# An adaLN transformer block on one core: the feed-forward's modulation moved from TensorE to VectorE, the first gate alone on TensorE, and the second half of x loaded ahead of the rotary tables

## The chip, the cores and the metric

The kernel runs on 1 core of a Trainium2 chip. The metric is the device time of one execution in microseconds (us). Five engines work beside each other, each through its own queue in order: TensorE (PE, and PEld for its weight loads), VectorE (DVE), ScalarE (ACT), GpSimd (POOL) and SyncE (SP), which issues most of the DMA transfers.

## The reference: what is computed

x is 2 x 1024 x 256 in float32 (two batches, 1024 tokens). A vector c per batch is turned into six rows of 256: shift, scale and gate for the attention (sa, ca, ga) and for the feed-forward (sb, cb, gb).

```
mod = (silu(c) @ wmod).reshape(2, 6, 1, 256)
sa, ca, ga, sb, cb, gb = (mod[:, n] for n in range(6))
ga = (2 * (ga >= 0) - 1) * maximum(abs(ga), 0.25)        # gb likewise
h = layernorm(x) * (1 + ca) + sa
x = x + ga * attention(h, Wq, bq, Wk, bk, Wv, bv, Wo, bo)  # 16 heads of 128, rotary, causal
h = layernorm(x) * (1 + cb) + sb
x = x + gb * ffn(h)                       # silu(gate) * up, then down; 704 hidden, integer weights
```

## The kernel before

Everything is float32 but the integer weights. Rows of x lie in 8 tiles of 128 tokens per batch. A *head* below is one of the 32 units (batch, group of two heads, head), numbered 0 to 31 as the loop `for n, u in enumerate(units)` (line 754) takes them; each has 8 *slots* `i`, one for each tile of 128 queries. The order of all work is written out by hand (`manual_schedule`, line 700), and each engine's queue runs in that order.

In a slot the loop issues, in this order: `shared_out` (one output product `py`, line 516, of an earlier head, whose sum into x is VectorE's line 519; `py` has one PSUM bank, so the next `py` waits for that sum); `score` (the products `ps`, line 429, and VectorE's mask and row maximum `nmax`, line 432); `turned` (VectorE transposes the probabilities of the slot before into `t`, line 463; after every fourth tile SyncE issues 16 transfers that make `pT` of them, line 475); `expo` (ScalarE's exp, line 449); `release` (the rotary sums that the slot before has held back: VectorE's line 402 and GpSimd's line 405); `project_qk` in slots 1, 3, 4, 5 (the next head's q and k, line 386, ScalarE's r1, line 398, GpSimd's product with the sine table, line 399); `values` (the products `po` of probabilities and v, line 490, copied out by ScalarE, line 498: for the first 512 queries of the head before in slot 0, but in slot 2 while n is 1, for its last 512 in slots 6 and 7); `project_v` in slots 0 and 2 (two tiles of v, line 368, copied out by ScalarE, line 375); and `extras`, where everything else is put into a slot by hand: `fold_out` (GpSimd scales Wo by the gate of the attention, lines 337 to 341, in slot 2 of even heads), loads by ScalarE's queue (the second batch's x, the feed-forward's weights `raw` and scales `s_bc`), VectorE's conversion of these weights (line 280), the layernorm of the second batch and of the feed-forward.

Before the loop stands the start. The transfers of the first inputs are issued in the order c (ScalarE's queue), x tiles 0 to 3, the attention's modulation weights `wmod` in two halves, the gates' weights `wga`, Wq and Wk of the first group, the first halves of the rotary tables, x tiles 4 and 5, Wv, x tiles 6 and 7, the second halves of the tables, the feed-forward's modulation weights, the weights of the next group. Some matmuls on ones (`warm_ps`) run ahead. TensorE then makes the attention's shift and scale as columns (`modulation(0)`: 16 matmul records `pm`, line 123), transposes the first four normalized tiles of x (`ptx`, line 216), which VectorE and ScalarE write to `hT` with shift and scale (lines 224 and 222), and makes q, k and v of head 0; the second four tiles follow. `gates_product` (line 147) makes the rows of both gates, 512 wide, its two terms in two places behind the transposes; `gates` (lines 153 to 162) clamps them on VectorE, writes them to DRAM and reads them back into all partitions. The feed-forward's shift and scale are made by `modulation(2)` in slot 7 of head 0, `wmod`'s second half being loaded by then.

Tiles of one tag share buffers: tag `f` has two, which hold first `wmod` and `wga`, then `s_bc` and `raw`, then others. `bw` (fold_out's small tile) has two.

Of the kernel before, what the change touches and what calls it, by code (L numbers as in the profile page):

```python
# [37 lines left out]
def adaln_block(ctx: ExitStack, tc: tile.TileContext, a, cos_d, sin_d, out):  # L38
# [20 lines left out]

    wmod = fpool.tile([P, 2, 2, KC, D], F32, tag="f", name="wmod")  # L60
    wga = fpool.tile([P, KC, 2 * D], F32, tag="f", name="wga")

    def load_x(b, t, n, eng):
        eng.dma_start(x[b][:, t : t + n, :], x_d[b, :, t : t + n, :])

    def load_wmod(block, n, eng):
        eng.dma_start(wmod[:, block, n], a["L0_wmod"][block, n])


    row_c = rot.tile([P, QB], F32, tag="r1", name="row_c")[: B * KC, :P]  # L70
    nc.scalar.dma_start(row_c, a["L0_c"])
    load_x(0, 0, 1, nc.sync)
    load_x(0, 1, 3, nc.sync)
    for n in range(2):
        load_wmod(0, n, nc.sync)

# [37 lines left out]

    def modulation(which, pool, tag):

        pm = pool.tile([P, 512], F32, tag=tag, name=f"pm{which}")

        wide = pm.rearrange("p (n f r b) -> p n f r b", n=2, f=KC, b=B)
        for n in range(2):  # L120
            for f in range(KC):
                for k in range(KC):
                    nc.tensor.matmul(  # L123
                        wide[:, n, f],
                        wmod[:, which // 2, n, k, ts(f, P)],
                        sc[:, :, k].unsqueeze(1).to_broadcast([P, P // B, B]),
                        start=(k == 0),
                        stop=(k == KC - 1),
                    )
        pms[which] = wide  # L130

    pms = {}

    def shift_scale(which):
        pm = pms[which]
        for n in range(2):
            nc.vector.tensor_scalar(modT[:, which + n], pm[:, n, :, 0, :], float(n), None, ALU.add)

    dram = pool("dram", 1, space=bass.MemoryType.DRAM)
    grow_d = dram.tile([B, 2 * D], F32, name="grow_d")  # L140

    pgs = []

    def gates_product(k):
        if k == 0:
            pgs.append(ps_y.tile([P, 512], F32, tag="y", name="pg"))
        nc.tensor.matmul(pgs[0][:B], sc[:, :, k], wga[:, k, :], start=(k == 0), stop=(k == KC - 1))  # L147

    def gates():

        pg = pgs.pop()
        sgn = ppool.tile([P, S], F32, tag="p", name="sgn")[:B, :QB]
        nc.vector.tensor_scalar(sgn, pg[:B], 0.0, 2.0, ALU.is_ge, ALU.mult)
        mag = ppool.tile([P, S], F32, tag="p", name="mag")[:B, :QB]
        nc.vector.tensor_scalar(mag, pg[:B], -1.0, None, ALU.mult)
        nc.vector.scalar_tensor_tensor(mag, pg[:B], 0.25, mag, ALU.max, ALU.max)
# [543 lines left out]
    with tc.manual_schedule():  # L700
        pc = ps_a.tile([P, 512], F32, tag="a", name="pc")
        nc.tensor.transpose(pc[:, : B * KC], row_c, ident[: B * KC, : B * KC])
        for n in range(2):
            warm_up(4)
        nc.scalar.activation(sc.rearrange("p b k -> p (b k)"), pc[:, : B * KC], AF.Silu)
        nc.scalar.activation(warm, eps_t, AF.Sqrt)
        weights[0, 0] = {}
        nc.sync.dma_start(wga, a["w_gates"])
        load_w(0, 0, "q")
        load_w(0, 0, "k")  # L710
        for t, t_d in ((cos_t, cos_d), (sin_t, sin_d)):
# [19 lines left out]
        modulation(0, ps_o, "o")  # L731
        nc.scalar.dma_start(cols, a["biases"])
        ln_scale(0, "a", 0, (0, 1))
        ln_scale(0, "a", 0, (2, 3))
        shift_scale(0)
        ln_turn(0, "a", 0, 0, new_hT(0, 0), split=True)
        gates_product(0)
        for t in range(4, NT):
# [15 lines left out]
        for n, u in enumerate(units):  # L754
            b, g, h = u
            prev = units[n - 1] if n else None
            nxt = units[n + 1] if n + 1 < N else None
            nb, ng = (b, g + 1) if g + 1 < NG else (b + 1, 0)
            more = nb < B
            for i in range(NT):  # L760

                shared_out(8 * n + i - 13)
                if owed:
                    owed.pop()()
                ps, nmax = score(u, i)
                if i >= 1:
                    turned(u, i - 1)
                elif prev:
                    turned(prev, NT - 1)
                expo(u, i, ps, nmax)  # L770
                release()
                if i in (1, 3, 4, 5) and nxt:
                    project_qk(nxt, *{1: ("q", 0), 3: ("k", 0), 4: ("q", 1), 5: ("k", 1)}[i])
                if i in (6, 7) and prev:
                    values(prev, 1, 4 * (i - 6), 4 * (i - 5))
                if i in (0, 2):
                    if h == 0:
                        project_v(b, g, 4 + i, *((ps_a, "a") if n else (ps_o, "o")))
                    elif more:
                        project_v(nb, ng, i)  # L780
                if not nxt and i in filler:
                    hidden(0, 0, filler.index(i), late=False, hold=True)

                if prev and i == (0 if n > 1 else 2):
                    values(prev, 0, 0, 4)
                extras(n, i)
                if i == 7 and h == 1:
                    if more:
                        load_out(nb, ng)
                    if n + 3 < N:  # L790
                        load_proj(*units[n + 3][:2])
# [119 lines left out]
```

## Time and profile before

| | |
|---|---|
| median of 3 runs | 1072.07 us (1071.98 to 1072.41) |
| the profiled execution | 1071.95 us |
| its span, from the first instruction to the last | 1070.2 us |
| start of head 0, 1, 2, 3 on TensorE | 23.13, 42.99, 70.56, 99.83 us |
| length of most heads from then on | 29.27 us |
| VectorE, ScalarE, GpSimd busy in head 2 (29.27 us) | 18.02, 14.35, 14.68 us |
| DMA | 132.02 MB in all, mean 123 GB/s |

A group of the profile reads: line of the kernel, engine, operation, what it writes <- what it reads, partitions x elements; then busy time and the mean of one in ns. In a timeline the first two numbers are the start and the length in us from the span's start, and a bracket at the end holds the engine's idle time before the instruction and what ended it. Matmuls are pipelined, so their records overlap. One product of float32 makes two records. Lengths of a head on TensorE are taken from the starts of its first `ps`.

### The profile page before, as it was taken

Reading aid. Unit: us, or ns where it says so; the run is one execution under the profiler, and the core shown is the slowest. Engines: PE = TensorE matmul, PEld = TensorE weight load, DVE = VectorE, ACT = ScalarE, POOL = GpSimd, SP = SyncE. Lnnn points to the kernel's source line nnn. Section 1 sums busy time; section 2 is a strip of 40 time slices with the busy share of each in tenths; the row PEclk is TensorE's granted clock in tenths of the full one; section 3 lists DMA queues with packets and bytes.
Section 4 is the critical chain, followed back from the end, with each engine's and each line's share of the span. In section 5 each row is a group of like instructions: output and inputs, shape, how many; then the busy total and the mean of one; then the engine's idle time right before and its main releaser. Section 6 shows DMA issues by size and latency. Waiting matters only on the chain.

```text
span 1070.2 us, 12390 instructions
## 1 busy us (share of the span) xinstructions
PE 1066.2 (100%) x3513; PEld 638.2 (60%) x3513; DVE 655.2 (61%) x1427; ACT 507.8 (47%) x956; POOL 398.8 (37%) x368
## 2 busy tenths in 40 slices
PE   9999999999999999999999999999999999999998
PEld 5665655666665655555666666656555666545747
DVE  5665675665667776665776556656767856555321
ACT  5654454554445444544544444544555544562120
POOL 4735353534343343754333444334343333200100
PEclk9999999999999999999999999999999999999999
DMA  6465656656565555566564656454555656423201
GB/s 227 104 159 126 159 120 141 156 126 148 119 150 115 142 119 134 120 148 163 111 148 109 148 116 148 101 138 99 144 121 116 148 129 138 110 50 77 71 1 39
DMA packets 68047, 132.02 MB, mean 123 GB/s; under 512 B 19302, under 2 KB 23402, under 8 KB 67980
## 3 DMA queue, kind: packets, MB, share of 16 engines
q1 hardware_dynamic: 66340, 126.96, 50.1%
q10 hardware_dynamic: 1592, 4.16, 1.2%
q8 instruction: 28, 0.46, 0.2%
q14 instruction: 39, 0.32, 0.1%
q0 software_dynamic: 48, 0.13, 0.1%
HBM read 25.26 MB, written 2.10 MB: 26 GB/s over the span
## 4 chain that ended last, share of the span: by engine, by line
PE 100%; issue 0%; DVE 0%; POOL 0%; POOLq 0%
PE po L490 23%; PE ps L429 23%; PE py L516 10%; PE pv L368 10%; PE pq L386 10%; PE pk L386 10%; PE pgu L545 7%; PE pd L603 2%; PE pd_0w L603 1%; PE pd_1w L603 1%; PE warm_ps L86 1%; PE pm L123 0%; PE pd L592 0%; PE pg L147 0%; PE ptx_a L216 0%; PE pd_1r L603 0%
## 5 line engine op out<-in xcount | busy, mean ns | idle before, releaser
L449 ACT ACTIVATE p<-ps,nmax 128x128 f32<-128x128 f32 (+7 forms) x256 | 189.8, 741 | 343.1 <-DVE nmax L432 342.9
L429 PE MATMUL ps<-kT,qT 128*128 128x512 f32 (+3 forms) x768 | 289.5, 486 | 0.0
L432 DVE CUSTOM_DVE_ANT_0 ps<-ps,mask 128x128 f32<-128x128 f32 (+7 forms) x256 | 195.6, 764 | 114.4 <-PE ps L429 113.6
L490 PE MATMUL po<-pT,v 128*128 128x512 f32 (+3 forms) x768 | 263.6, 486 | 0.0
L519 DVE SCALAR_TENSOR_TENSOR x<-py,rden,x 128x256 f32<-128x256 f32 x256 | 122.9, 481 | 224.5 <-PE py L516 220.9
L490 PEld LDWEIGHTS po<-pT,v 128*128 128x128 f32 x768 | 145.7, 190 | 123.4 <-issue 92.8
L399 POOL TENSOR_TENSOR r_q<-r_q,sin_t 128x512 f32<-128x512 f32 x64 | 81.9, 1279 | 362.5 <-ACT r_q L398 360.4
L463 DVE STREAM_TRANSPOSE t<-p 128x128 f32<-128x128 f32 (+7 forms) x256 | 198.2, 774 | 3.6 <-DMA pT<-t 1.8
L429 PEld LDWEIGHTS ps<-kT,qT 128*128 128x128 f32 x768 | 145.7, 190 | 77.6 <-issue 64.1
L516 PE MATMUL py<-wo,o 128*128 128x256 f32 x512 | 151.2, 380 | 0.0
L516 PEld LDWEIGHTS py<-wo,o 128*128 128x128 f32 x512 | 92.6, 190 | 77.6 <-issue 52.6
L368 PE MATMUL pv<-wv,hT 128*128 128x256 f32 x512 | 121.1, 379 | 0.0
L386 PE MATMUL pq<-hT,wq 128*128 128x512 f32 x256 | 120.5, 593 | 0.0
L386 PE MATMUL pk<-hT,wk 128*128 128x512 f32 x256 | 120.3, 592 | 0.0
L368 PEld LDWEIGHTS pv<-wv,hT 128*128 128x128 f32 x512 | 94.8, 190 | 19.5 <-issue 1.3
L399 POOL TENSOR_TENSOR r_k<-r_k,sin_t 128x512 f32<-128x512 f32 x64 | 81.5, 1273 | 64.5 <-ACT r_k L398 64.3
L405 POOL TENSOR_TENSOR kT<-kT,r_k 128x512 f32<-128x512 f32 x64 | 81.2, 1268 | 56.5 <-DVE kT L402 41.6
L398 ACT ACTIVATE r_q<-pq,cols 64x512 f32<-64x512 f32 x128 | 87.4, 683 | 21.9 <-PE pq L386 19.6
L405 POOL TENSOR_TENSOR qT<-qT,r_q 128x512 f32<-128x512 f32 x64 | 83.4, 1303 | 33.6 <-DVE qT L402 30.9
L398 ACT ACTIVATE r_k<-pk,cols 64x512 f32<-64x512 f32 x128 | 87.4, 683 | 5.9 <-PE pk L386 0.4
L386 PEld LDWEIGHTS pk<-hT,wk 128*128 128x128 f32 x256 | 48.6, 190 | 48.0 <-issue 45.0
L386 PEld LDWEIGHTS pq<-hT,wq 128*128 128x128 f32 x256 | 46.2, 190 | 33.1 <-issue 30.6
(104 smaller groups left out, 686.7 us busy)
## 6 DMA issues: line engine op xcount, KB each, us to landing
pT<-t SPq DMA_DIRECT2D x512, 128.0 KB, 2.4
pT<-t SPq DMA_DIRECT2D x512, 64.0 KB, 2.0
wq<-in_Wq SPq DMA_DIRECT2D x16, 256.0 KB, 3.1
wk<-in_Wk SPq DMA_DIRECT2D x16, 256.0 KB, 4.0
wv<-in_Wv SPq DMA_DIRECT2D x16, 256.0 KB, 4.3
wo<-in_Wo SPq DMA_DIRECT2D x16, 256.0 KB, 2.8
out<-yo SPq DMA_DIRECT2D x15, 128.0 KB, 1.8
wmod<-in_wmod SPq DMA_DIRECT2D x4, 256.0 KB, 4.6
```

The lines of the kernel that those rows point to most:

```text
L368: nc.tensor.matmul(pv[:, ts(j, HG * DH)], hT[b, n][:, k, ts(r, P)], weights[b, g]["v"][:, k, :], start=(k == 0), stop=(k == KC - 1),)
L386: nc.tensor.matmul(pq, weights[b, g][s][:, k, ts(h, DH)], hT[b, n][:, k, :], start=(k == 0), stop=(k == KC - 1),)
L398: nc.scalar.activation(r1[to], pq[of], AF.Identity, bias=cols[of, c : c + 1])
L399: nc.gpsimd.tensor_tensor(r1, r1, sin_t[:, sl], ALU.mult)
L405: nc.gpsimd.tensor_tensor(dst[:, sl], dst[:, sl], r1, ALU.add)
L429: nc.tensor.matmul(ps[:, c:e], qT[:, ts(i, P)], kT[:, c:e], start=True, stop=True)
L432: nc.vector.tensor_tensor_reduce(ps[:, :L], ps[:, :L], mask[:, NT - 1 - i :, :].rearrange("p t k -> p (t k)"), -SCALE, FLT_MAX, ALU.add, A ...
L449: nc.scalar.activation(p[:, :L], ps[:, :L], AF.Exp, bias=nmax, scale=-1.0, accum_out=dens[u][:, i : i + 1])
L463: nc.vector.transpose(t32[blk][:, :, j, : i + 1, :].rearrange("p c k b -> p k c b"), p[:, : (i + 1) * P].rearrange("p (k c a) -> p k c a", ...
L490: nc.tensor.matmul(po[:, off * P :], vs[b, g][:, k, ts(h, DH)], pT[:, off:, :, k, :], start=(k == 0), stop=(k == last),)
L516: nc.tensor.matmul(py[:, :D], outs[u][:, ts(t, P)], weights[b, g]["o"][:, h, :], start=True, stop=True)
L519: nc.vector.scalar_tensor_tensor(x[b][:, t, :], py[:, :D], rdens[u][:, t : t + 1], x[b][:, t, :], ALU.mult, ALU.add)
```

## The change

The attention's modulation (shift and scale) stays with TensorE; its weights and the weights of the first gate are one tile of three parts. The first gate's row is made alone (`gate_a`): 256 wide, both terms in the first of the two places. For the feed-forward, silu(c) is written to DRAM as a row by GpSimd's queue and read back into all partitions; `late_load` (slot 7 of head 1, ScalarE's queue) brings that and the weights, turned so that an output column is a row of 256 in each partition. `late_column` makes one column of shift, scale or gate for both batches with two multiply-and-sum reductions on VectorE, in slots 3 and 5 of heads 2, 3 and 4. The second gate is clamped as columns (`gate_b`, head 5), turned by one transpose on TensorE (`gate_b_turn`, head 6), and spread over the partitions (head 7).

In the order of loads, x tiles 4 to 7 stand ahead of the rotary tables, and Wv behind the tables' first halves; the second batch's x and the feed-forward's weights are loaded in other heads. The v products of group 1 move: two of the four from heads 1 and 2 into slots 6 and 7 of head 0. The first `values` of head 2 go to slot 2.

```diff
-    wmod = fpool.tile([P, 2, 2, KC, D], F32, tag="f", name="wmod")
-    wga = fpool.tile([P, KC, 2 * D], F32, tag="f", name="wga")
+    wmod = fpool.tile([P, 3, KC, D], F32, tag="f", name="wmod")
...
-    def load_wmod(block, n, eng):
-        eng.dma_start(wmod[:, block, n], a["L0_wmod"][block, n])
-    row_c = rot.tile([P, QB], F32, tag="r1", name="row_c")[: B * KC, :P]
+    def load_wmod(n):
+        nc.sync.dma_start(wmod[:, n], a["L0_wmod"][n])
+    row_c = small.tile([P, D], F32, tag="bw", name="row_c", bufs=2)[: B * KC, :P]
...
-    def shift_scale(which):
-        pm = pms[which]
+        return wide
...
-    grow_d = dram.tile([B, 2 * D], F32, name="grow_d")
-    pgs = []
-    def gates_product(k):
-        if k == 0:
-            pgs.append(ps_y.tile([P, 512], F32, tag="y", name="pg"))
-        nc.tensor.matmul(pgs[0][:B], sc[:, :, k], wga[:, k, :], start=(k == 0), stop=(k == KC - 1))
-    def gates():
...
+    crow_d = dram.tile([1, B * D], F32, name="crow_d")
+    grow_d = dram.tile([2, B, D], F32, name="grow_d")
+    late = {}
+    def gates(sgn, mag, pg):
...
-        nc.sync.dma_start(grow_d, mag)
+    def gate_rows(n):
         for b in range(B):
-            for m, n in enumerate(("a", "b")):
-                nc.sync.dma_start(
-                    gate[n, b], grow_d[b : b + 1, m * D : (m + 1) * D].to_broadcast([P, D])
-                )
+            row = grow_d["ab".index(n), b : b + 1, :]
+            nc.sync.dma_start(gate[n, b], row.to_broadcast([P, D]))
+    def gate_a():
+        pg = ps_y.tile([P, 512], F32, tag="y", name="pg")[:B, :D]
+        for k in range(KC):
+            nc.tensor.matmul(pg, sc[:, :, k], wmod[:, 2, k, :], start=(k == 0), stop=(k == KC - 1))
+        def rest():
+            sgn = ppool.tile([P, S], F32, tag="p", name="sgn")[:B, :D]
+            mag = ppool.tile([P, S], F32, tag="p", name="mag")[:B, :D]
+            gates(sgn, mag, pg)
+            nc.sync.dma_start(grow_d[0], mag)
+            gate_rows("a")
+        return rest
+    def late_load():
+        t = fpool.tile([P, (3 * KC + B) * D], F32, tag="f", name="late_mod")
+        late["w"] = t[:, : 3 * KC * D].rearrange("p (n f k) -> p n f k", n=3, f=KC)
+        late["c"] = t[:, 3 * KC * D :].rearrange("p (b k) -> p b k", b=B)
+        nc.scalar.dma_start(t[:, 3 * KC * D :], crow_d.to_broadcast([P, B * D]))
+        nc.scalar.dma_start(late["w"], a["late_mod"])
+        late["g"] = const.tile([P, B, KC], F32, name="gcol")
+    def late_column(n, f):
+        for b in range(B):
+            junk = xnp.tile([P, D], F32, tag="xn", name=f"junk{n}{f}{b}")
+            to = modT[:, 2 + n, f, b : b + 1] if n < 2 else late["g"][:, b, f : f + 1]
+            nc.vector.tensor_tensor_reduce(
+                junk, late["w"][:, n, f], late["c"][:, b], 1.0, float(n == 1), ALU.mult, ALU.add, to
+            )
+    def gate_b():
+        g = late["g"].rearrange("p b f -> p (b f)")
+        sgn = small.tile([P, B * KC], F32, tag="sgn", name="sgn_b", bufs=1)
+        mag = small.tile([P, B * KC], F32, tag="mag", name="mag_b", bufs=1)
+        gates(sgn, mag, g)
+        late["mag"] = mag
+    def gate_b_turn():
+        mag = late["mag"]
+        pt = ps_o.tile([P, 512], F32, tag="o", name="pgb")[: B * KC, :P]
+        nc.tensor.transpose(pt, mag, ident)
+        rows_ = small.tile([P, D], F32, tag="bw", name="grow", bufs=2)[: B * KC, :P]
+        nc.scalar.copy(rows_, pt)
+        nc.sync.dma_start(grow_d[1].rearrange("b (f p) -> (b f) p", p=P), rows_)
...
         if i == (2 if n else 7) and units[n][2] == 0:
             fold_out(*units[n][:2])
-        if n == 0 and i == 7:
-            modulation(2, ps_y, "y")
-            shift_scale(2)
+        if n == 1 and i == 7:
+            late_load()
+        if n in (2, 3, 4) and i in (3, 5):
+            late_column(n - 2, i // 4)
+        if n == 5 and i == 3:
+            gate_b()
+        if n == 6 and i == 3:
+            gate_b_turn()
+        if n == 7 and i == 3:
+            gate_rows("b")
...
-        for m, name in ((3, "gate"), (5, "up"), (6, "last")):
+        for m, name in ((5, "gate"), (6, "up"), (7, "last")):
             if n == m and i == 7:
                 ffn_weight_load(name)
             if n == m + 1 and i in (2, 5):
                 ffn_weight_scale(name, i // 4)
-        if n in (0, 4, 6, 8) and i == 7:
-            load_x(1, max(0, n - 2), 2, nc.scalar)
+        if n in (3, 4, 8, 9) and i == 7:
+            load_x(1, {3: 0, 4: 2, 8: 4, 9: 6}[n], 2, nc.scalar)
...
+        nc.scalar.activation(row_c, row_c, AF.Silu)
         nc.scalar.activation(warm, eps_t, AF.Sqrt)
+        nc.gpsimd.dma_start(crow_d.rearrange("o (r p) -> (o r) p", p=P), row_c)
         weights[0, 0] = {}
-        nc.sync.dma_start(wga, a["w_gates"])
+        load_wmod(2)
         load_w(0, 0, "q")
         load_w(0, 0, "k")
+        load_x(0, 4, 2, nc.sync)
+        load_x(0, 6, 2, nc.sync)
         for t, t_d in ((cos_t, cos_d), (sin_t, sin_d)):
             nc.sync.dma_start(t[:, :QB], t_d[:, :QB])
-        load_x(0, 4, 2, nc.sync)
         load_w(0, 0, "v")
-        load_x(0, 6, 2, nc.sync)
         for t, t_d in ((cos_t, cos_d), (sin_t, sin_d)):
             nc.sync.dma_start(t[:, QB:], t_d[:, QB:])
-        for n in range(2):
-            load_wmod(1, n, nc.sync)
         load_proj(*units[2][:2])
         load_out(0, 0)
         nc.gpsimd.memset(bvacc, 0.0)
...
         ln_turn(0, "a", 0, 0, new_hT(0, 0), split=True)
-        gates_product(0)
+        gate_a_rest = gate_a()
...
         ln_turn(0, "a", 1, 0, new_hT(0, 1), split=True, wide=True)
-        gates_product(1)
         project_v(0, 0, 2, ps_sc, "sc", S)
-        gates()
+        gate_a_rest()
...
                 if i in (0, 2):
-                    if h == 0:
-                        project_v(b, g, 4 + i, *((ps_a, "a") if n else (ps_o, "o")))
+                    if n in (1, 2):
+                        if i == 0:
+                            project_v(0, 1, 2 + 2 * n)
+                    elif n == 0:
+                        project_v(b, n, 4 + i, ps_o, "o")
+                    elif h == 0:
+                        project_v(b, g, 4 + i)
                     elif more:
                         project_v(nb, ng, i)
+                if n == 0 and i in (6, 7):
+                    project_v(0, 1, 2 * (i - 6))
...
-                if prev and i == (0 if n > 1 else 2):
+                if prev and i == (0 if n > 2 else 2):
                     values(prev, 0, 0, 4)
                 extras(n, i)
...
     wmod = v["L0_wmod"].reshape(D, 2, 3, D)
-    args["L0_wmod"] = given("in_wmod", by_partition(np.moveaxis(wmod[:, :, :2], 0, 2), 2))
-    args["w_gates"] = given("in_w_gates", by_partition(wmod[:, :, 2].reshape(D, 2 * D)))
+    args["L0_wmod"] = given("in_wmod", by_partition(np.moveaxis(wmod[:, 0], 0, 1), 1))
+    late_mod = wmod[:, 1].reshape(D, 3, KC, P)
+    args["late_mod"] = given("in_late_mod", late_mod.transpose(3, 1, 2, 0))
```

More of the change, by code (lines that the diff above doesn't have):

```diff
@@ L74, in adaln_block @@
     for n in range(2):
-        load_wmod(0, n, nc.sync)
+        load_wmod(n)
     ident = const.tile([P, P], F32, name="ident")
@@ L113, in adaln_block, with modulation @@
     bvacc = const.tile([P, D], F32, name="bvacc")
-    def modulation(which, pool, tag):
-        pm = pool.tile([P, 512], F32, tag=tag, name=f"pm{which}")
+    def modulation(pool, tag):
+        pm = pool.tile([P, 512], F32, tag=tag, name="pm")
         wide = pm.rearrange("p (n f r b) -> p n f r b", n=2, f=KC, b=B)
@@ L124, in modulation @@
                         wide[:, n, f],
-                        wmod[:, which // 2, n, k, ts(f, P)],
+                        wmod[:, n, k, ts(f, P)],
                         sc[:, :, k].unsqueeze(1).to_broadcast([P, P // B, B]),
@@ L129, in modulation, with shift_scale @@
                     )
-        pms[which] = wide
-    pms = {}
-    def shift_scale(which):
-        pm = pms[which]
+        return wide
+    def shift_scale(pm):
         for n in range(2):
-            nc.vector.tensor_scalar(modT[:, which + n], pm[:, n, :, 0, :], float(n), None, ALU.add)
+            nc.vector.tensor_scalar(modT[:, n], pm[:, n, :, 0, :], float(n), None, ALU.add)
     dram = pool("dram", 1, space=bass.MemoryType.DRAM)
-    grow_d = dram.tile([B, 2 * D], F32, name="grow_d")
-    pgs = []
@@ L144, in gates_product @@
-    def gates_product(k):
-        if k == 0:
-            pgs.append(ps_y.tile([P, 512], F32, tag="y", name="pg"))
-        nc.tensor.matmul(pgs[0][:B], sc[:, :, k], wga[:, k, :], start=(k == 0), stop=(k == KC - 1))
-    def gates():
[L151 to L156, printed above, removed]
+    crow_d = dram.tile([1, B * D], F32, name="crow_d")
@@ L157, in gates @@
+    grow_d = dram.tile([2, B, D], F32, name="grow_d")
+    late = {}
+    def gates(sgn, mag, pg):
+        nc.vector.tensor_scalar(sgn, pg, 0.0, 2.0, ALU.is_ge, ALU.mult)
+        nc.vector.tensor_scalar(mag, pg, -1.0, None, ALU.mult)
+        nc.vector.scalar_tensor_tensor(mag, pg, 0.25, mag, ALU.max, ALU.max)
         nc.vector.scalar_tensor_tensor(mag, sgn, -1.0, mag, ALU.add, ALU.mult)
-        nc.sync.dma_start(grow_d, mag)
+    def gate_rows(n):
         for b in range(B):
-            for m, n in enumerate(("a", "b")):
-                nc.sync.dma_start(
-                    gate[n, b], grow_d[b : b + 1, m * D : (m + 1) * D].to_broadcast([P, D])
-                )
+            row = grow_d["ab".index(n), b : b + 1, :]
+            nc.sync.dma_start(gate[n, b], row.to_broadcast([P, D]))
@@ L730, in adaln_block @@
             ln_sqrt(0, "a", t, t + 2)
-        modulation(0, ps_o, "o")
+        pm = modulation(ps_o, "o")
         nc.scalar.dma_start(cols, a["biases"])
@@ L734, in adaln_block @@
         ln_scale(0, "a", 0, (2, 3))
-        shift_scale(0)
+        shift_scale(pm)
         ln_turn(0, "a", 0, 0, new_hT(0, 0), split=True)
-        gates_product(0)
+        gate_a_rest = gate_a()
         for t in range(4, NT):
```

## The prediction, made before the result was known

> **What bounds the kernel now.** First the page: busy times and the chain that ended last.
>
> ```profile
> PE 1066.2 (100%) x3513; PEld 638.2 (60%) x3513; DVE 655.2 (61%) x1427; ACT 507.8 (47%) x956; POOL 398.8 (37%) x368
> PE 100%; issue 0%; DVE 0%; POOL 0%; POOLq 0%
> ```
>
> TensorE is busy throughout and the whole chain is TensorE. Since its records overlap, I read the distance from one start to the next, not the length of a record. A 512-column record follows its predecessor by 0.429 us nearly everywhere, a 256-column one by 0.216 and a 128-column one by 0.11: TensorE runs without gaps after the first 23 us. So a matmul taken away is worth its start-to-start time, and work on another engine is free until TensorE waits for it. Next comes TensorE's timeline at the places that the change touches (start, length, line):
>
> ```profile
> 9.61 1.02 PE L147 MATMUL pg<-wga,sc 128*2 128x512 f32 x2
> 10.56 1.98 PE L386 MATMUL pq<-hT,wq 128*128 128x512 f32 x4
> ...
> 15.82 1.17 PE L216 MATMUL ptx_a<-ident,xn_a 128*128 128x128 f32 x8
> 16.92 1.02 PE L147 MATMUL pg<-wga,sc 128*2 128x512 f32 x2
> 17.87 1.99 PE L368 MATMUL pv<-wv,hT 128*128 128x256 f32 x8
> 19.70 1.88 PE L386 MATMUL pq<-hT,wq 128*128 128x512 f32 x4
> ...
> 41.20 1.95 PE L123 MATMUL pm<-sc,wmod 128*128 128x128 f32 x16
> 42.99 0.39 PE L429 MATMUL ps<-kT,qT 128*128 128x128 f32 x2
> ```
>
> The two gate products take 0.95 us each from start to next start, the second modulation 1.79. The pq at 19.70 needs the second block of hT, so VectorE's timeline of the start comes third:
>
> ```profile
> 9.28 0.81 DVE L224 TENSOR_SCALAR hT<-ptx_a,modT 128x512 f32<-128x512 f32 x1 [0.21 <-PE ptx_a L216]
> 11.46 0.43 DVE L186 BATCH_NORM_STATS2 st_a<-x 128x6 f32<-128x256 f32 x1 [1.37 <-DMA x<-in_x]
> ...
> 14.79 1.38 DVE L202 TENSOR_SCALAR xn_a<-x,mv_a,rstd_a 128x256 f32<-128x256 f32 x4
> ...
> 17.98 0.80 DVE L224 TENSOR_SCALAR hT<-ptx_a,modT 128x512 f32<-128x512 f32 x1
> ```
>
> VectorE waits 1.37 us for the second half of x. ScalarE writes the other half of hT from 18.82 to 19.60, and pq starts at 19.70: TensorE's queue and this chain end together, so removing the gate product alone would bring nothing here.
>
> **The sum.** The profiled execution took 1071.95 us: 1070.2 of span and 1.75 around it. The median shown is 1072.07.
>
> *Second modulation, -1.79.* Its 16 records at the end of head 0 go. The two v products that now stand in slots 6 and 7 there (8 records, 1.73 us each) come out of heads 1 and 2, so TensorE's total does not change by them; head 0 grows by 3.46 - 1.79, heads 1 and 2 shrink by 1.73 each.
>
> *Gate product, -1.2.* At 9.61 four 256-column records (0.86) take the place of two 512-column ones: nothing, and pq stays at 10.56. The second place goes. TensorE's queue would then reach pq at 15.82 + 8 x 0.11 + 1.73 = 18.43, or 18.62 if the 0.09 and 0.10 us by which neighbours of pg start late stay with the transposes; 18.5. Can hT follow? x tiles 4 and 5 come after as many bytes as wk did (2.1 MB), which landed at 9.40; tiles 6 and 7 some 0.7 later. VectorE is free at 10.09. Four statistics at 0.57 end at 12.4, ScalarE's root at 12.75, xn runs from 13.05 to 14.45. ScalarE's r_q and r_k (0.69 a half) follow root and pk: 12.75 to 14.15 and 14.3 to 15.7. VectorE's kT waits for r_k: 15.7 to 16.45. The transposes now start at 15.82 without the 0.13 us that they waited for xn, hT's first half ends at 17.25 and ScalarE's at 18.05. That is 0.45 before 18.5, so 19.70 becomes 18.5. Bounds: -1.27 and, if hT is not earlier, 0. I take -1.2, as the bytes say.
> What is moved behind stays covered: the tables come after 2.9 MB (wv's place was 3.1 MB, 12.2) and land by 11.5, needed at 14.15; wv keeps its byte count; the second tables have two loads fewer ahead. SP issues each transfer in 0.33 to 0.5 us and stays ahead of them. ScalarE's added Silu (0.17 to 0.3, the Silu and root rows) fits its 0.95 idle before 6.08, GpSimd's added DMA issue (0.73, bo_bc's row) its 11.6 idle before 15.96.
>
> *Transpose of the second gate, +0.40.* One 128-column record (0.11). Around pg, with 2 columns of weights, the records before, at and behind the change of width start 0.09, 0.09 and 0.10 late; this one has 4 columns. Bounds 0.11 and 0.56 (its neighbours' record is 0.27 long). Its mag was made a head earlier. ScalarE's copy waits for GpSimd's sum of bw in that head, which in head 6 ends at 200.85; the copy's turn comes behind r_k at 201.8.
> [...]
>
> *Columns on VectorE, 0.* Twelve reductions over 128x256: 0.43 + 0.14 for the accumulator by the nmax rows of this size, bounds 0.38 (sd, two SBUF inputs) and 1.85 (with a whole GpSimd operation of 1.28 waited for). Two come after slot 3 and two after slot 5 of heads 2 to 4. The room, in head 2:
>
> ```profile
> 82.16 0.57 DVE L463 STREAM_TRANSPOSE t<-p 128x384 f32<-128x384 f32 x1
> 83.69 0.48 DVE L519 SCALAR_TENSOR_TENSOR x<-py,rden,x 128x256 f32<-128x256 f32 x1 [0.96 <-PE py L516]
> 84.77 0.83 DVE L432 CUSTOM_DVE_ANT_0 ps<-ps,mask 128x640 f32<-128x640 f32 x1 [0.59 <-PE ps L429]
> ```
>
> Behind the pair wait x's add and, through its single bank, the next py at 86.29. From 82.73 to 86.29 less the add's 0.48 are 3.08 us, and the pair takes 1.14. After slot 5 the room is about 4.0 (90.57 to py at 95.09). Uncovered, all twelve would cost 6.8. gate_b's four 128x4 operations (0.15) hide likewise; the narrower first gate gives VectorE back 1.2 where it idled 2.04 anyway.
>
> *Late loads, 0.* 1 MB by ScalarE's queue at the end of head 1 (two issues of 0.33). The nearest row is raw's 640 KB at 128.96: SP's transfers of pT were held for 3.1 us, the last landed at 146.12, po read it at 150.21. With 1.6 times the bytes the hold is 5.0, and head 2 is 1.73 shorter before that po: 4.1 - 1.9 - 1.73 leaves 0.5. The moved x and weight loads land as far before their use as now, one to a head. Queue SP: the row of gate b (head 6) and its two broadcasts (head 7, 0.42 each) stand ahead of pT's transfers, in slots in which SP waits for turned probabilities (111.5 to 115.5 in head 3).
>
> *Head 0's new v products* take ps_a banks: pq of head 1's slot 1 needs the bank that ScalarE empties behind the last exp, near 45.25; TensorE gets there at 45.85.
>
> Sum: -1.79 - 1.2 + 0.40 = -2.6, 1069.35 from the profiled execution, 1069.47 from the median: 1069.5.
>
> **The rivals.** *B, the loads land no earlier* (the change doesn't do what it says): pq stays near 19.6. Sum -1.4 - 0.1: 1070.6. For it: hT has only 0.45 to spare, and cols, issued at 7.14, landed at 12.42, just ahead of the new r_q. Against: wk's landing. 0.14.
>
> *C, GpSimd delays the columns, or pT is late.* [...]
>
> ```profile
> 138.55 0.92 DVE L280 SCALAR_TENSOR_TENSOR wgateT<-raw,s_bc 128x640 f32<-128x640 int32 x1
> ```
> ```profile
> 138.87 1.73 POOL L405 TENSOR_TENSOR qT<-qT,r_q 128x512 f32<-128x512 f32 x1
> ```
>
> An operation with two SBUF inputs ran, and GpSimd's next one took 1.73 instead of 1.27; xn at 344.14 took 1.22 instead of 0.41 beside GpSimd. If each column waits for a whole operation, a pair takes 3.7, 0.62 more than the room after slot 3: 3 x 0.62 = 1.9, 1071.4. A late pT in head 2 would cost about as much. 0.16.
> [...]
>
> [...] 0.08.
>
> **The numbers.** Forecast A, 1069.5 (1069.0 to 1069.9): 0.62. A measurement of this kernel tells 0.2% (2.1 us, 1069.93) from no change; A lies beyond that, B and C within it: faster 0.62, same 0.30, slower 0.08. The range takes A with the lower bounds of its terms, B and C: 1068.9 to 1071.5.
>
> **What would show it.** In the new profile: second pq near 18.5, head 0's first ps near 21.9, head 1 near 43.5, head 2 near 69.3, head 7 near 214.3 (216.93 now). Wrong would be: VectorE's statistics still waiting near 11 (B); py in slot 5 of heads 2 to 4 starting late behind columns of over 1 us (C, D); the first po of slot 6 in head 2 behind a DMA (C); more than 0.6 us around the transpose.

## The result and the profile after

The changed kernel takes 1070.12 us (median of 17 runs, 1069.29 to 1071.57), the kernel before 1072.15 on the same chip (17 runs, 1071.92 to 1073.58): a ratio of 0.998, 95% interval 0.9973 to 0.9988, so 1.3 to 2.9 us less. Its profiled execution took 1070.12 us with a span of 1068.3; before it was 1071.95 and 1070.2. The two lines of the page that were shown of before now read:

```profile
PE 1063.9 (100%) x3498; PEld 636.4 (60%) x3498; DVE 662.6 (62%) x1453; ACT 509.3 (48%) x958; POOL 400.4 (37%) x369
PE 98%; DMA 1%; ACT 0%; SPq 0%; DVE 0%; issue 0%; ACTq 0%
```

TensorE has 2.3 us less work, VectorE 7.4 more. The chain that ended last was TensorE alone; now 1% of it is DMA, and the same view's list by line names two transfers, cols (the biases) and Wq. Starts on TensorE, in us from the span's start (a head's start is its first `ps`):

| | before | after | difference |
|---|---|---|---|
| first pm | 6.85 | 6.90 | +0.05 |
| first pq | 10.56 | 10.86 | +0.30 |
| second pq | 19.70 | 19.39 | -0.31 |
| head 0 | 23.13 | 22.89 | -0.24 |
| head 2 | 70.56 | 70.24 | -0.32 |
| head 3 | 99.83 | 97.94 | -1.89 |
| head 7 | 216.93 | 215.14 | -1.79 |
| head 31 | 920.25 | 918.46 | -1.79 |

Head 1 is left out, since products moved across its start; the removed second modulation shows only once heads 0 to 2 are over. From head 0 to head 3 the gain grows by 1.65, from head 6's transpose on 0.10 is given back, and behind that nothing changes. Two places fall short, the start and head 2. TensorE at the start:

```profile
9.90 1.02 PE L157 MATMUL pg<-wmod,sc 128*2 128x256 f32 x4
10.86 1.98 PE L423 MATMUL pq<-hT,wq 128*128 128x512 f32 x4
...
16.12 1.04 PE L253 MATMUL ptx_a<-ident,xn_a 128*128 128x128 f32 x8
16.99 1.89 PE L405 MATMUL pv<-wv,hT 128*128 128x256 f32 x8
19.39 1.96 PE L423 MATMUL pq<-hT,wq 128*128 128x512 f32 x4 [0.50 <-DVE hT L261]
```

The second gate product is gone and TensorE would be ready some 0.66 earlier: pq now stands 8.53 behind the first pq where 9.14 less 1.27 would be 7.87. The bracket says that it waited for hT. ScalarE's timeline tells why:

```profile
8.49 0.36 ACTq L776 DMA_DIRECT2D cols<-in_biases  x1
10.01 0.78 ACT L259 ACTIVATE hT<-ptx_a,modT 128x512 f32<-128x512 f32 x1 [2.19 <-PE ptx_a L253]
12.91 0.30 ACT L228 ACTIVATE rstd_a<-mv_a,eps_t 128x4 f32<-128x4 f32 x1 [2.12 <-DVE mv_a L224]
14.94 1.38 ACT L435 ACTIVATE r_q<-pq,cols 64x512 f32<-64x512 f32 x2 [1.73 <-DMA cols<-in_biases]
...
19.27 0.78 ACT L259 ACTIVATE hT<-ptx_a,modT 128x512 f32<-128x512 f32 x1 [0.92 <-DVE hT L261]
```

The root (`rstd_a`) is 1.26 earlier than before (14.17), as x's second half now comes early. But r_q, which adds a bias from cols, waits 1.73 us for that transfer, and r_k, VectorE's kT and hT follow it in turn. cols was issued at 7.14 before and landed at 12.42; now it is issued at 8.49 and lands at 14.86. The last line is ScalarE's half of hT: TensorE's pq has started by then (19.39), as its first product reads VectorE's half alone.

In head 2, VectorE shows the second place:

```profile
89.42 0.84 DVE L500 STREAM_TRANSPOSE t<-p 128x640 f32<-128x640 f32 x1 [2.24 <-DMA pT<-t]
90.19 0.71 DVE L439 SCALAR_TENSOR_TENSOR qT<-pq,cols,cos_t 128x512 f32<-128x512 f32 x1
90.82 0.41 DVE L182 CUSTOM_DVE_ANT_0 junk<-late_mod 128x256 f32<-128x256 f32 x1
...
91.16 1.48 DVE L182 CUSTOM_DVE_ANT_0 junk<-late_mod 128x256 f32<-128x256 f32 x1
...
92.57 0.47 DVE L556 SCALAR_TENSOR_TENSOR x<-py,rden,x 128x256 f32<-128x256 f32 x1
```

The transpose into t must wait until the 16 transfers of pT have read the old t. That takes until 89.4, the pair of columns follows late, one of them 1.48 long beside GpSimd, and x's add ends behind the point at which TensorE wants the next py. SyncE's own waits between 60 and 100 us name what held those transfers, whose last was issued at 86.63:

```profile
SPq L512 <- DMA late_mod<-in_late_mod: 2.6, 1, 2.6
SPq L512 <- DMA late_mod<-crow_d: 2.4, 1, 2.4
```

The columns are us in total, times, longest: two waits, 5.0 us together, for the two late loads (256 KB and 768 KB; the second was issued at 70.44 and landed at 80.36). The three transfers of pT that SyncE issued ahead of these waits, at 72.35 to 73.55, did not land before 80.68 to 81.86 either. In this execution the py at 93.10 comes 0.155 us late by all this.

So the profiled execution: -0.24 at the start, -1.79 for the modulation, +0.155 in head 2, +0.10 at the transpose; that is -1.78, and -1.83 was measured.

### The profile page after: what moved, and what is told of

It is laid out like the page before. It is cut to its first block, busy times and chain, and to the rows that moved or that the text cites. A ratio compares the mean times of both kernels' runs of the same rounds, so it can differ in the third digit from the quotient of the medians.

```text
span 1068.3 us, 12393 instructions
## 1 busy us (share of the span) xinstructions
PE 1063.9 (100%) x3498; PEld 636.4 (60%) x3498; DVE 662.6 (62%) x1453; ACT 509.3 (48%) x958; POOL 400.4 (37%) x369
## 4 chain that ended last, share of the span: by engine, by line
PE 98%; DMA 1%; ACT 0%; SPq 0%; DVE 0%; issue 0%; ACTq 0%
PE po L527 23%; PE ps L466 23%; PE py L553 10%; PE pq L423 10%; PE pk L423 10%; PE pv L405 10%; PE pgu L582 7%; PE pd L640 2%; PE pd_0w L640 1%; PE pd_1w L640 1%; DMA cols<-in_biases 1%; DMA wq<-in_Wq 1%; PE pd L629 0%; ACT r_k L435 0%; ACT r_q L435 0%; SPq L66 0%
## 5 line engine op out<-in xcount | busy, mean ns | idle before, releaser
L466 PEld LDWEIGHTS ps<-kT,qT 128*128 128x128 f32 x768 | 145.8, 190 | 77.4 <-issue 64.1
L435 ACT ACTIVATE r_q<-pq,cols 64x512 f32<-64x512 f32 x128 | 87.6, 684 | 23.5 <-PE pq L423 19.6
```

The costliest lines, as they stand in the source:

```text
L435: nc.scalar.activation(r1[to], pq[of], AF.Identity, bias=cols[of, c : c + 1])
L466: nc.tensor.matmul(ps[:, c:e], qT[:, ts(i, P)], kT[:, c:e], start=True, stop=True)
```

## The experiments

*Theory.* The change's mechanism holds (a modulation and a gate product less on TensorE, the columns hidden). What it fails to gain is lost to two transfers: cols at the start, and the 1 MB of late loads in head 2, whose hold varies from execution to execution and so makes most of the spread of 2.3 us. *Rival at the start:* x's second half is not early enough, or TensorE's own queue is the bound and the gate's removal is worth less. *Rivals in head 2:* the columns beside GpSimd are late by themselves; or it is SyncE's wait behind a foreign transfer, not the bytes.

**The same kernel again.** No edit.

> The changed kernel as it is, beside the next three on one chip. 1070.1 us, with executions between 1069.3 and 1071.5. In its profile ScalarE's first r_q waits for the biases' transfer (cols) to about 14.9 us, and the second pq of head 0's q starts near 19.4.

1069.51 us (9 runs, 1069.10 to 1070.12), ratio 0.9974 (0.9964 to 0.9984): the ratio lies within the interval above, and the median is 0.6 lower. r_q waits 1.81 us for cols; x tiles 1 to 3 landed at 5.29 (5.77 in the execution above) and the first pq started at 10.38, so 0.5 us of the start is decided by when the first bytes come, and differs between executions of one kernel. Head 2 lost 0.36.

**cols ahead.** The transfer is issued at the top of the start instead of behind the first modulation:

```diff
+    nc.scalar.dma_start(cols, a["biases"])
...
-        nc.scalar.dma_start(cols, a["biases"])
```

> The biases' transfer (cols, 24 KB) is issued right behind the modulation weights at the very start, nothing else changes. Theory 'cols': that transfer, put behind 2.9 MB by the new order, is what kept the start from getting shorter. r_q then starts at about 13.2, hT's second half is done at 18.4, the second pq starts at 18.7 instead of 19.4, and the time is 0.6 to 0.7 us lower, 1069.4, with a narrower spread. Rival 'hT is late for another reason' (x's second half, or ScalarE's and VectorE's own work): second pq stays at 19.3 to 19.4, time within 0.2 us of e1.

1069.53 us (11 runs, 1068.96 to 1072.43), ratio 0.9979 (0.997 to 0.9987). cols lands at 5.95, r_q starts at 13.58 right behind the root, and from first to second pq it is 7.87 us without a wait: exactly TensorE's own queue. So the hold at the start was cols. The time didn't fall as expected, though: the median is that of the run above, and the slowest run is slower. The first pq is at 10.85, as x tiles 1 to 3 land at 5.76; and the spread stays, as does VectorE's wait for pT in head 2 (1.68 us, which cost TensorE nothing in the profiled execution).

**x's second half in its old place**: tiles 4 and 5 behind the tables' first halves, 6 and 7 behind Wv.

```diff
-        load_x(0, 4, 2, nc.sync)
-        load_x(0, 6, 2, nc.sync)
...
+        load_x(0, 4, 2, nc.sync)
         load_w(0, 0, "v")
+        load_x(0, 6, 2, nc.sync)
```

> The changed kernel with x tiles 4 to 7 back in their old places: 4 and 5 behind the first rotary tables, 6 and 7 behind Wv. Theory 'cols': moving x ahead is what delayed cols, so undoing it lets cols land near 12.5 again; statistics then end near 13.5 and r_q starts near 13.9 instead of 14.9; 0.3 to 0.6 us lower than e1. Rival 'x ahead is what the start gained': statistics late, r_q not before 14.5 to 15, 0.3 to 1.0 us higher than e1.

1069.80 us (9 runs, 1068.84 to 1071.17), ratio 0.9967 to 0.9986 (0.9977). By the median alone, 0.3 over the changed kernel's second measurement, the rival would stand; the profile decides against it. With x in its old place the second pq follows the first by 7.87, and head 0 starts at 21.82, 1.07 earlier than in the changed kernel (0.34 of it since the first pq was earlier). cols, with fewer bytes ahead, is issued at 8.16 and lands at 13.10, before the root. The profiled execution then lost 1.99 us in head 2 (29.53 us long, against 27.54 where nothing disturbs), most of it with TensorE itself at a stop for pT:

```profile
90.25 3.67 PE L527 MATMUL po<-pT,v 128*128 128x512 f32 x8 [1.29 <-DMA pT<-t]
```

That is the changed kernel's head 2 on a worse day: the late loads landed at 81.07 there. They were late for the columns of slot 3 as well: VectorE waited 1.60 us for them, and TensorE lost 0.26 of the 1.99 from the py behind them on.

**The late loads a head and a half earlier.**

```diff
-        if n == 1 and i == 7:
+        if n == 0 and i == 2:
             late_load()
```

> late_load in slot 2 of head 0 (few transfers run there) instead of slot 7 of head 1; the columns stay where they are. Theory 'the 1 MB held SP's transfers of pT': VectorE's wait of 2.2 us for pT in head 2 goes, and with it the 0.15 us by which a py of head 2 was late; 0.15 us lower than e1, too little for the timing alone, to be read in the profile. Rival 'the columns and GpSimd made that py late': the wait of VectorE goes or not, but the py after slot 5 of head 2 is still late by 0.1 us or more.

1069.10 us (7 runs, 1068.89 to 1069.52), ratio 0.9971 (0.996 to 0.9982). The spread is 0.6 where the changed kernel's was 2.3, and it stays under 0.7 in every kernel below with the loads in this place. (The kernel before, without such loads, has two of 17 runs some 1.6 us above its fastest, so they are not the only thing that can spread a time.) VectorE's line for the same transpose in head 2 has no bracket, and SyncE's longest waits there are for turned probabilities, none for a late load:

```profile
86.34 0.84 DVE L500 STREAM_TRANSPOSE t<-p 128x640 f32<-128x640 f32 x1
...
88.08 1.48 DVE L182 CUSTOM_DVE_ANT_0 junk<-late_mod 128x256 f32<-128x256 f32 x1
...
89.49 0.47 DVE L556 SCALAR_TENSOR_TENSOR x<-py,rden,x 128x256 f32<-128x256 f32 x1
```
```profile
SPq L512 <- DVE t L500: 9.4, 3, 5.6
```

The 1.48 us column is still there and costs nothing: x's add ends at 89.96, py is due at 92.34. So the columns beside GpSimd were not late by themselves; head 2 was late because of the loads. From head 0 to head 3 it is 74.89 us, 1.81 less than before.

**Both early** (cols and late loads).

> cols issued at the very start and late_load in slot 2 of head 0, together. Theory 'two transfers spoil two places': the start is then set by TensorE's queue alone (second pq 7.87 us behind the first, as in e2 and e3) and head 2 has no wait (as in e4): 1068.8 us, with executions within about 0.6 us of each other. Rival 'only one of them matters': no lower than e4 (1069.1) by more than 0.1.

1069.24 us (7 runs, 1069.13 to 1069.55), ratio 0.9972 (0.9961 to 0.9983). No wait is left, and yet it isn't under the 1069.10 without cols' move, as the rival said: the second pq follows by 7.87, but the first pq starts at 10.77 with x tiles 1 to 3 landed at 5.67. In the four kernels with cols ahead, the two with repeated columns below included, these tiles landed at 5.60 to 5.76, in seven executions of the others at 5.29 to 5.56. It looks as if cols holds up x by about as much as it gains later; three executions without that move (5.59, 5.65, and the changed kernel's 5.77) forbid calling it shown. There was also less to gain than 0.66: in the run before this one, with cols late, the second pq followed the first by 8.07, only 0.20 over TensorE's own queue.

**x in its old place, late loads early** (the edits of the two sections above together).

> x tiles 4 to 7 in their old places and late_load in slot 2 of head 0; cols stays behind. If x ahead is worth something by itself, this is slower than e4 (1069.1) by 0.3 us or more. By the theory it is faster than e4 by 0.2 to 0.3: cols lands about 1.1 us earlier without the 0.5 MB of x ahead of it, statistics end at 13.4, r_q starts near 13.7 and the second pq 7.9 us behind the first.

1069.01 us (8 runs, 1068.87 to 1069.23), ratio 0.997 (0.9959 to 0.998): the lowest median of all, by 0.09 only under the run with the late loads alone moved, whose interval overlaps, so the 0.2 to 0.3 of the theory is not seen in the time. It faces neither hold. Its slowest run lies under the fastest of the changed kernel's 17 (1069.29), if not of the nine taken again (1069.10). The start on TensorE:

```profile
10.45 1.98 PE L423 MATMUL pq<-hT,wq 128*128 128x512 f32 x4
...
18.31 1.88 PE L423 MATMUL pq<-hT,wq 128*128 128x512 f32 x4
```

7.86 us against 9.14 before: the gate product and its neighbours' delays were worth 1.28. Moving x ahead of the tables brings nothing: in their old place tiles 4 and 5 land at 10.73 where it was 11.43 before; 256 KB fewer stand ahead of them (the first gate's weights alone instead of both gates').

**Each column made twice, and four times** (the kernel with both early; the same results, written again).

```diff
-        for b in range(B):
+        for b in [b for b in range(B) for _ in range(2)]:
```

> e5 with each of the twelve columns computed twice (the second result over the first): four reductions a slot instead of two. By the room of 3.08 us behind slot 3 four at 0.49 (1.96) fit, with one GpSimd operation waited for (1.0) just so: within 0.3 us of e5. Rival 'the columns are near the edge already': a py late behind them in every one of the six slots, 1 us or more in all.

> e5 with each column computed four times: eight reductions a slot, 3.9 us without waits, some 5 to 6 with GpSimd's operations between. By the room (3.08 behind slot 3, 4.0 behind slot 5) TensorE waits 1 to 3 us in each of the six slots: 6 to 15 us over e5. If VectorE has more room than that account says: under 3 us over e5.

Twice: 1069.27 us (7 runs, 1069.10 to 1069.59) against 1069.24: four reductions a slot, 1.48 us long at worst, still hide. Four times: 1083.18 us (one run), 13.9 over the kernel with both early. TensorE waits for x's add in slots 3 and 5 of heads 2, 3 and 4, by 1.4 to 3.3 us from start to start after slot 3 and by 0.6 to 1.5 after slot 5. One of these waits cost more than its length. In head 2:

```profile
86.29 0.67 PE L554 MATMUL py<-wo,o 128*128 128x256 f32 x2 [2.79 <-DVE x L557]
86.80 2.29 PE L467 MATMUL ps<-kT,qT 128*128 128x512 f32 x4
88.89 2.78 PE L424 MATMUL pk<-hT,wk 128*128 128x512 f32 x4
```
```profile
86.30:91.00 4.70, 4.70 (x9) 2.52 (x10) 4.28 (x10) 3.00 (x5) 2.49 (x2) 0.64 0.24 56
```

The pk of four records is 2.78 long instead of 1.88, and in the second fence (the stretch, its length, busy time and instructions of PE, PEld, DVE, ACT and POOL, then the granted clock) the clock is 0.64 of full speed: over 4.70 us a loss of 1.69 (4.70 x 0.36, an estimate). The starts agree: from this ps to pk it is 2.09 us and from pk to the next py (91.50) 2.61, where the run with the late loads alone moved has 1.29 and 1.72. So some 1.7 us came on top of the wait.

**The late loads by GpSimd's queue**, so that SyncE's transfers share nothing with ScalarE's:

```diff
-        nc.scalar.dma_start(t[:, 3 * KC * D :], crow_d.to_broadcast([P, B * D]))
-        nc.scalar.dma_start(late["w"], a["late_mod"])
+        nc.gpsimd.dma_start(t[:, 3 * KC * D :], crow_d.to_broadcast([P, B * D]))
+        nc.gpsimd.dma_start(late["w"], a["late_mod"])
```

> The changed kernel with its two late loads (1 MB, slot 7 of head 1) issued by GpSimd's queue instead of ScalarE's; the bytes and the place stay. Theory 'SP waits for them': SP's transfers share a round of semaphores with ScalarE's, and it was these waits (3.0 and 3.5 us in e3's head 2) that held pT; now SP goes on, VectorE's wait for pT in head 2 falls from 2.2 to 3.6 us to under 1, TensorE doesn't wait, 1069.2 us and a narrow spread as in e4. Rival 'the DMA engines are full': pT lands as late as before, waits of 1.5 us or more in head 2, times spread to 1070 and beyond.

1069.50 us (6 runs, 1068.91 to 1069.91), ratio 0.9971 (0.9959 to 0.9982). SyncE waits for no late load and head 2 has no stall. But GpSimd reached the two issues at 65.80, 4.3 us before ScalarE did, and the loads landed at 73.24. Queue and time changed together, so the next run put the time back: GpSimd first copies a small tile that is final at the end of head 1.

```diff
+        gone = small.tile([P, NT], F32, tag="gone", name="gone", bufs=1)
+        nc.gpsimd.tensor_scalar(gone, dens[units[1]], 1.0, None, ALU.mult)
```

> e9 issued its loads at 65.8 us, 4.3 earlier than the changed kernel, since GpSimd had nothing before them; that mixes place and queue. Here GpSimd first copies a tile that ScalarE's last exp of head 1 completes, so that the loads are issued near 70.2 us, by GpSimd's queue. Theory 'SP waits for them': SP has no wait on them, VectorE waits under 1 us for pT in head 2 and TensorE not at all; 1069.3, spread as in e9. Rival 'bytes in the engines': pT is late by 2 us or more although SP waits for nothing, and TensorE waits in head 2 by 0.1 to 1.5 us. If the loads themselves come too late, VectorE waits for late_mod in front of slot 3's columns, and py in slot 5 is late.

1070.67 us (11 runs, 1069.53 to 1071.61), ratio 0.9983 (0.9974 to 0.9992): the loss and its spread are back. Issued from 70.29 on, the loads landed at 82.27, and head 2 lost 1.13 us on TensorE. SyncE's, VectorE's and TensorE's lines show where:

```profile
SPq L514 <- DMA pT<-t: 4.5, 1, 4.5
```
```profile
82.40 0.68 DVE L184 CUSTOM_DVE_ANT_0 junk<-late_mod 128x256 f32<-128x256 f32 x1 [2.15 <-DMA late_mod<-in_late_mod]
...
89.97 0.84 DVE L502 STREAM_TRANSPOSE t<-p 128x640 f32<-128x640 f32 x1 [2.02 <-DMA pT<-t]
```
```profile
84.50 0.67 PE L555 MATMUL py<-wo,o 128*128 128x256 f32 x2 [0.52 <-DVE x L558]
```

Most of the loss, 0.97 us, is one that the changed kernel's profiled execution didn't have and the expectation named last: VectorE waits 2.15 us for the late loads themselves in front of slot 3's columns, and py waits for x's add behind them. The other 0.16 is the loss through pT, 0.155 in the changed kernel. pT's first eight transfers, now issued without a wait for a late load, are slow themselves (issued from 71.9 to 77.4, landed from 82.6 to 85.1; for the ninth SyncE waits 4.5 us, until the first has landed), and VectorE waits about as long as before. So my theory that SyncE's wait behind ScalarE's transfer was the cause falls: pT is late without it. What the runs leave is 1 MB beside pT and the next weights at that time, by either queue. The loads took 11.4 us from issue to landing here and 9.3 to 11.7 in four executions by ScalarE's queue; what they share with pT that makes both slow stays open.

**The gate product twice** (the kernel of the lowest median, with a second, unread product behind the second transposes, where before had its second term):

```diff
...
+        for k in range(KC):
+            nc.tensor.matmul(
+                late["pg"][:B, D:], sc[:, :, k], wmod[:, 2, k, :], start=(k == 0), stop=(k == KC - 1)
+            )
```

> e6 with the first gate's product made a second time (into an unread half of its bank) in the place behind the second transposes where the second half of the gates' product stood before the change. If TensorE's queue alone sets the start now, the second pq starts 0.86 us later for the four records, and 0.2 to 0.3 more if a product with 2 columns of weights holds up its neighbours: 0.9 to 1.15 us over e6 (1069.0). If hT were still the bound, less than 0.5.

1070.19 us (10 runs, 1070.04 to 1070.56), ratio 0.998 (0.997 to 0.9989): 1.18 more than without, on another chip. In the profile it is 9.02 from pq to pq, 1.16 more, which is four 256-column records of 0.215 and the three delays of 0.09, 0.09 and 0.10. So without a hold the start is bound by TensorE's queue, and a gate product is worth its price.

**What narrow weights cost** (the same kernel of the lowest median, with one unread 256-column product in slot 3 of heads 20, 22 and 24, its weights 2, 4 and 128 columns wide):

```diff
+        if n in (20, 22, 24) and i == 3:
+            some = {20: sc[:, :, 0], 22: late["mag"], 24: ones}[n]
+            wide = ps_o.tile([P, 512], F32, tag="o", name=f"probe{n}")[: some.shape[1], :D]
+            nc.tensor.matmul(wide, some, bvacc, start=True, stop=True)
```

> e6 with one product over 256 columns (two records, unread) added in slot 3 of three heads where TensorE waits for nothing: 2 columns of weights in head 20, 4 in head 22, 128 in head 24. Prediction's row for the gate's transpose: the records at and around a narrow product start 0.09, 0.09 and 0.10 late. By it heads 20 and 22 grow by 0.7 us and head 24 by 0.43. If narrow weights cost nothing (the transpose's 0.10 us in all), each grows by 0.43. If it is 2 columns alone, 0.7, 0.43 and 0.43.

1071.09 us (one run). In head 20 (2 columns):

```profile
606.18 1.88 PE L423 MATMUL pk<-hT,wk 128*128 128x512 f32 x4
607.99 0.59 PE L697 MATMUL probe<-bvacc,sc 128*2 128x256 f32 x2
608.52 0.70 PE L553 MATMUL py<-wo,o 128*128 128x256 f32 x2
609.05 1.24 PE L466 MATMUL ps<-kT,qT 128*128 128x512 f32 x4
```

From the probe's start back to pk's it is 1.81 instead of 1.72, to py 0.53 and from py to ps 0.53 instead of 0.43. The product costs 0.725 us, and 0.725 with 4 columns, but 0.43 with 128: with 2 or 4 columns of weights it cost 0.29 more. The transpose of gate b, whose weights are 4 columns wide as well, shows nothing of it:

```profile
198.26 0.27 PE L197 MATMUL pgb<-ident,mag_b 128*4 128x128 f32 x1
198.37 0.60 PE L553 MATMUL py<-wo,o 128*128 128x256 f32 x2
```

The next record follows by 0.11 us. What spares the transpose stays open: it is one record, a product of float32 two, and no run told that apart.

## Why the prediction was right, and where not

*Direction and size.* 1069.5 was forecast; 1070.12 and, again, 1069.51 were measured, and 1069.0 to 1069.3 once both holds were taken away. The first lies within the stated range, but above forecast A's own 1069.0 to 1069.9, and its gain of 2.0 us falls just short of the 2.1 that the prediction asked of a measurement (the 17 runs of each kernel do tell the two apart). Part of the nearness is luck: the gate's term promised 0.96 too much and head 2's loss of 0.155 was missing, but the transpose's term charged 0.30 too much. Both removed pieces of TensorE's work were worth what the start-to-start times said. The missing part of up to 1.1 us comes from two transfers and, by up to 0.5, from when the first bytes land.

*Second modulation, -1.79.* Right: -1.81 from head 0 to head 3 where nothing disturbs, -1.65 with the 0.155 of head 2 in it.

*Gate product, -1.2.* TensorE's half of the step was right (-1.28 measured, -1.27 as the bound). The sentence that failed is "ScalarE's r_q and r_k (0.69 a half) follow root and pk: 12.75 to 14.15". The root ended at 13.2, but r_q started at 14.94, because cols was late. I looked at every load that the change moved and asked if it came early enough, and held the one that it didn't touch at its old 7.14 and 12.42 (it stands so in rival B). Yet cols is issued behind another transfer on the semaphore it was given: before, that was the second transfer of `wmod`, landed at 6.73, so at 7.14 it was free; in the changed order cols shares one with Wq's first transfer, and in all nine executions in which cols keeps this place it is issued 0.02 to 0.03 us after Wq's landing (8.49 after 8.46 here). With cols ahead it is x tiles 6 and 7 that share one with cols, and they go out 0.02 us after its landing (5.97 after 5.95). In the changed order cols then takes 6.4 us to land behind the bytes that now stand ahead (4.9 with x in its old place). Of the 1.27, 0.66 went there (0.20 to 0.68 in the five executions with cols behind x), and 0.30 by the time of the first pq, which varies between executions. "If hT is not earlier, 0" was the other bound; what happened lies between them. Rival B came nearer (pq near 19.6, 1070.6) and had the right object in cols, but not the right cause: x did land earlier.

A reading underneath was wrong too: that pq waits for ScalarE's half of hT, so that TensorE's queue and this chain end together and "removing the gate product alone would bring nothing here". In the changed kernel pq started at 19.39, 0.15 after VectorE's half was done, with ScalarE at work on the other half until 20.05. Before, VectorE's half was done at 18.78 and pq started at 19.70. By these rows some 0.7 us were to be had without moving x (an estimate), and with x in its old place the whole 1.28 came.

*Transpose, +0.40.* Too high; 0.10 was measured, the lower bound of 0.11. The row of pg that I took the neighbours' delays from is a product with 2 columns of weights, and in the probe products with 2 and 4 columns did pay 0.29; the transpose, with 4, doesn't.

*Columns, 0.* Right, by the mechanism named. They took 0.38 to 0.50 plus 0.08 for the accumulator (0.43 and 0.14 forecast), up to 1.48 beside GpSimd, and were hidden; even twice as many were. The sign named for C and D, a py behind slot 5 late after a column of over 1 us, did appear (0.155), but went with the late loads' move while the column stayed as long. Four times as many cost 14 us, so the cover is real and ends between four and eight reductions a slot. The 0.08 stood for D, a slower kernel whose columns wait through a whole run of GpSimd's operations: no run shows such a wait, and with one pair a slot the longest column of head 2 took 1.49 us.

*Late loads, 0.* This step was too near its edge: "leaves 0.5". The hold's size was right (5.0 estimated; 2.4 + 2.6 measured, and 4.3 to 6.5 in three further executions). What I left out is that po is not the only one to wait: VectorE's transpose needs the old t to have been read by the same transfers, and behind it stand qT, the pair of columns, x's add and py. That chain made py 0.155 late here; in another execution po itself stood still for 1.29. It is rival C's second half, "A late pT in head 2 would cost about as much" (1.9); head 2 lost between 0 and 2.0 us, differing from one execution to the next. Nor did I ask when the loads must land for the first column: here it was 80.36 for a column at 80.61, and in two other executions they came too late. Both losses vanish when the loads are moved, and most of the spread with them.

## What to carry to other kernels

When loads are put in another order, list those that are *not* moved too: a small transfer that was just in time may sit behind more bytes, or behind a transfer whose semaphore it shares (here cols, 24 KB, was issued at 8.49 instead of 7.14 and landed at 14.86 instead of 12.42). A change that adds a large load beside a stream of transfers with deadlines should be put where that stream is idle: here a move by a head and a half took the slowest run from 1071.57 to 1069.52 us, and issuing it by another queue at the same time brought nothing (1070.67 us). And where the times of one kernel spread by more than another's (2.3 us against 0.6 with the loads moved), look for a transfer whose landing races a consumer.

## What was not expected of the hardware

Behind a wait of 2.79 us in head 2 (each column made four times) TensorE's granted clock was 0.64 over 4.70 us, while in the same run it stayed 1.00 from 140 to 156 us, around a wait of 3.12 us in head 4: the four-record pk behind that one is 1.98 long, not 2.78. So the length of a wait alone did not decide it; what did was not shown.

The price of narrow weights, 0.29 us around a 2- or 4-column product (0.725 against 0.43) and nothing around a 4-column transpose, was measured and is not explained. And in slot 5 of the changed kernel's head 2 VectorE's reduction with two SBUF inputs took 0.41 us at 90.82, with GpSimd idle, and 1.48 at 91.16, beside GpSimd's product for qT (91.05 to 92.36); the second column there took the same 1.48 or 1.49 in all eleven kernels with one pair a slot: that cost repeats, it isn't chance.
